# Sums over heads taken for two groups at a time, in a six-layer attention stack on one core

## The chip, the cores and the metric

The kernel runs on one core of a Trainium2 chip. The metric is the device time of one execution in microseconds (us). Times of a kernel before and after a change are taken in turns on the same chip.

## The reference

Eight sequences of 512 positions with 128 features go through six layers, and then through a gated FFN. What one layer computes (H = 16 heads of 8 features, biases and the affine parts of the norms left in):

```python
q = (h @ wq.T + bq).reshape(bh, sl, H, DH)
k = (h @ wk.T + bk).reshape(bh, sl, H, DH)
scores = einsum('blhd,bmhd->bhlm', q, k) / sqrt(DH)
w_avg = softmax(scores, -1).mean(axis=1)          # mean over the 16 heads
new_w = softmax(w_avg + exp(-|l - m| / 16), -1)
sa = einsum('blm,bme->ble', new_w, h)
h1 = ln(h + sa, l1w, l1b)
h2 = ln(h1, l2w, l2b)
ff = relu(h2 @ w1.T + b1) @ w2.T + b2
h = ln(h2 + ff, l3w, l3b)
```

The stack's input is the normalised x, its output is added to x. The FFN of 128 to 512 features (silu gate, two 512x512 layers with gelu, back to 128) is then added too. All arithmetic is float32 in its inputs and outputs.

## The kernel before

A **unit** is one layer of one sequence: 6 x 8 = 48 units, in the order of the layers, so that a sequence comes back after eight units. A unit has 32 **steps** (`PAIRS`). In each step PE computes two blocks of scores, [128, 512] each (`ps`, one PSUM bank each, from a ring of six, L385); DVE takes the maximum of every row (`top`, L394); ACT the exponential with its row sum (`e`, `zs`, L399). A row of a block is one position and one head: 32 positions x 4 heads fill the 128 partitions.

Two steps make a **group** (`Group`): four blocks, one `e` tile, for 128 positions (`lc`) and four heads (`turn`). Four groups, eight steps, make the 16 heads of a query chunk. What follows for a group that began its second step at s:

- s + 2: DVE takes reciprocals of the row sums (`r`, L408), POOL spreads them into a [128, 32] weight for each block (`rp`, L410).
- s + 5: the **gather** (L420). Four float32 products, each in its own 32 columns of TensorE, sum each block of `e` over its four heads, weighted by `rp`, into the one PSUM tile `acc`. The four groups of a query chunk accumulate there.
- After the fourth group only: at s + 5 ACT takes the exponential of `acc` (`w`, `mix_exp`, L427); at s + 8 PE transposes it (`pt_w`, L193) and DVE multiplies it by the decay (`wT`, L437); at s + 10 PE multiplies it with h (`po`, L445), and DVE scales and adds h (L453, L454).

Counted in the unit's steps, gathers stand at every even step, `w` at 4, 12, 20, 28, `pt_w` at 7, 15, 23, 31, `po` at 1, 9, 17, 25.

The other work of neighbouring units is spread over the same steps by hand: `plan_before` (K and Q projections `pk`, `pq` at steps 3 and 5 with their ACT results `kT`, `qT`, splits, stacking by DMA on SP), `plan_after` (three norms, the hidden layer `pf` at 11, 13, 19, 21 with its relu `g`, L338, and the MLP output `py`, L348, in two halves at 27 and 29, each added to `z` by DVE, L355), and `plan_turns` (transposes `pt_h`, `pt_u` at the end of step 31, copied by ACT to `hT`, `uT`). `norm_c` is the norm of the sum with the MLP output: statistics of two chunks (L172), and of two more later. The steps of one unit's MLP lie two units after its scores.

The order on every engine is thus written out: `at(step, place, fn)` appends work to the list of an engine in a step, `first` puts it in front. Within a step PE gets its two scores, then the list; DVE its two maxima, then the list; ACT the list, then its two exponentials. Engines wait for each other by semaphores alone.

Buffers: `pk`, `pq`, `pf`, `py`, `pt_w` and `po` share one PSUM bank (`one`, pool `ps_one`). `e` has four tiles, the score ring six banks.

After the last unit come eight passes of the FFN (`gated`, one for each sequence, the next one's input prepared within it by `gated_in`), with the leftover steps of the last units between their parts.

Of the kernel before, what the change touches and what calls it, by code (L numbers as in the profile page):

```python
# [9 lines left out]
F32 = mybir.dt.float32  # L10
# [7 lines left out]
P = 128  # L18
# [3 lines left out]
QB = 32  # L22
# [7 lines left out]
def attn_stack_then_ffn(ctx: ExitStack, tc: tile.TileContext, a: dict, out: bass.AP):  # L30
    nc = tc.nc
    ctx.enter_context(tc.manual_schedule())
    x = a["x"]
    B, L, E = x.shape
# [4 lines left out]
    LC = L // P  # L39
    FC = F // P  # L40
    HC = HID // P
    NB = P // QB
# [4 lines left out]
    wts = ctx.enter_context(tc.tile_pool(name="wts", bufs=1))  # L47
    state = ctx.enter_context(tc.tile_pool(name="state", bufs=1))
    proj = ctx.enter_context(tc.tile_pool(name="proj", bufs=2))
    epool = ctx.enter_context(tc.tile_pool(name="e", bufs=4))  # L50
    work = ctx.enter_context(tc.tile_pool(name="work", bufs=2))
    small = ctx.enter_context(tc.tile_pool(name="small", bufs=6))
    ps_big = ctx.enter_context(tc.tile_pool(name="ps_big", bufs=6, space=PSUM))
# [39 lines left out]
    x_in = {}  # L93

    def load_x(b, n):
        t = state.tile([P, LC, E], F32, tag="x", name=f"x_{n}", bufs=3)
        nc.sync.dma_start(t, x[b].rearrange("(c p) e -> p c e", p=P))
        return t

# [90 lines left out]
    def transpose(pt, src):  # L190

        for c in range(LC):
            nc.tensor.transpose(pt[:, c * P : (c + 1) * P], src[:, c, :], ident)  # L193
# [10 lines left out]
    PAIRS = LC * STRIPS * 2  # L204

    class Unit:
# [12 lines left out]

        def turn_h(self, pt):  # L220
            transpose(pt, self.h[:, :, 0:E])
            self.hT = work.tile([P, L], F32, tag="hT", name=f"hT_{self.n}")
            return lambda: nc.scalar.copy(self.hT, pt)

        def project_k(self):
# [141 lines left out]
    class Group:  # L367
# [38 lines left out]
        def weights(self):  # L406
            r = small.tile([P, NB], F32, tag="r", name=f"r_{self.n}")
            nc.vector.reciprocal(r, self.zs)  # L408
            self.rp = small.tile([P, NB, QB], F32, tag="rp", name=f"rp_{self.n}", bufs=4)
            nc.gpsimd.tensor_tensor(  # L410
                self.rp,
                pick.unsqueeze(1).to_broadcast([P, NB, QB]),
                r.unsqueeze(2).to_broadcast([P, NB, QB]),
                ALU.mult,
            )
# [7 lines left out]
                )  # L423

        def mix_exp(self):
            self.w = work.tile([P, LC, P], F32, tag="w", name=f"w_{self.n}")
            nc.scalar.activation(  # L427
                self.w.rearrange("p c l -> p (c l)"), acc, AF.Exp, scale=1.0 / H
            )
# [31 lines left out]
    PE_, DVE_, ACT_, RING_ = range(4)  # L461
    later = {}

    def at(step, place, fn):
        later.setdefault((step, place), []).append(fn)

    def first(step, place, fn):
        later.setdefault((step, place), []).insert(0, fn)
# [11 lines left out]
    def norm_steps(base, un, make, s0, s1, s2, s3, s4):  # L480

        at(base + s0, DVE_, lambda: (make(), un.ln.stats(0, 2)))
        at(base + s1, DVE_, lambda: un.ln.stats(2, LC))
        at(base + s2, DVE_, lambda: un.ln.aggregate())
        at(base + s3, DVE_, lambda: un.ln.centre())
        at(base + s4, DVE_, lambda: un.ln.scale())
# [32 lines left out]
    def plan_after(un):  # L519

        s = (un.u + 1) * PAIRS
        norm_steps(s, un, un.norm_a, 11, 12, 13, 14, 15)
        at(s + 16, DVE_, lambda: un.affine_a(0))
        at(s + 17, DVE_, lambda: un.affine_a(1))
        norm_steps(s, un, un.norm_b, 19, 20, 22, 23, 24)
        at(s + 25, DVE_, lambda: un.affine_b(0))
        at(s + 26, DVE_, lambda: un.affine_b(1))
        s += PAIRS
        for f, step in enumerate((11, 13, 19, 21)):
            matmuls(s + step, lambda f=f: un.hidden(f))  # L530
        for half, step in enumerate((27, 29)):
            at(s + step, PE_, lambda half=half: un.mlp_out(half))
            at(s + step, DVE_, lambda half=half: un.mlp_add(half))
        norm_steps(s, un, un.norm_c, 28, 30, PAIRS, PAIRS + 9, PAIRS + 10)
        at(s + PAIRS + 11, DVE_, lambda: un.affine_c(0))
        at(s + PAIRS + 12, DVE_, lambda: un.affine_c(1))

    def plan_group(gr, s):

        first(s + 2, DVE_, gr.weights)  # L540
        first(s + 5, PE_, gr.gather)
        if gr.turn == STRIPS - 1:
            at(s + 5, ACT_, gr.mix_exp)
            at(s + 8, PE_, gr.mix_turn)
            at(s + 8, DVE_, gr.mix_decay)
            at(s + 10, PE_, gr.mix_values)
            at(s + 10, DVE_, gr.mix_end)
# [10 lines left out]
    for s in range(-2 * PAIRS, 0):  # L558
# [4 lines left out]
        step_rest(s)  # L563
        step_ring(s)

    for u, un in enumerate(obj):
        un.z1 = work.tile([P, LC, E], F32, tag="z1", name=f"z1_{un.n}")
        if u + 2 < B:
            x_in[u + 2] = load_x(u + 2, f"in{u + 2}")
        if un.b == 4 and un.d + 1 < D:  # L570
            load_layer(un.d + 1)
        if u == U - B:
            load_ffn()
            xs = {0: load_x(0, "out0")}
        if u + 2 < U:
            plan_before(obj[u + 2])
        plan_turns(u)
        plan_after(un)
        for pr in range(PAIRS):
            s = u * PAIRS + pr  # L580
            lc, turn, half = pr // 8, (pr // 2) % STRIPS, pr % 2
            if half == 0:
                gr = Group(un, lc, turn)
            peak, exps = gr.scores(half)
            if half == 1:
                plan_group(gr, s)
            pending(s, PE_)
            peak()
            pending(s, DVE_)
            pending(s, ACT_)  # L590
            exps()
            step_ring(s)
# [13 lines left out]
    def gated_in(b):  # L606

        xb = xs.pop(b)
        nc.gpsimd.tensor_tensor(xb, xb, hs[b][:, :, 0:E], ALU.add)
        if b + 1 < B:  # L610
            xs[b + 1] = load_x(b + 1, f"out{b + 1}")
        v = work.tile([P, LC, E], F32, tag="vf", name=f"v_{b}", bufs=1)
        ln = Norm(xb, v, f"f{b}")
        ln.stats(0, LC)
        ln.aggregate()
        ln.centre()
        ln.scale()
        yield
        vT = work.tile([P, L], F32, tag="hT", name=f"vT_{b}")
        pt = transposed(v, f"v{b}")  # L620
        nc.scalar.copy(vT, pt)  # L621
        ready[b] = (xb, vT)

    def gated(b):
        xb, vT = ready.pop(b)
        ahead = gated_in(b + 1) if b + 1 < B else iter(())
        gg = epool.tile([P, HC, L], F32, tag="e", name=f"fg_{b}")
        for o in range(HC):
            sl = slice(o * P, (o + 1) * P)
            p1, p2 = ring([P, L], f"p1_{b}_{o}"), ring([P, L], f"p2_{b}_{o}")  # L630
            nc.tensor.matmul(p1, fw1[:, sl], vT, start=True, stop=True)
            nc.tensor.matmul(p2, fw2[:, sl], vT, start=True, stop=True)
            sil = work.tile([P, L], F32, tag="w", name=f"sil_{b}_{o}")
            nc.scalar.activation(sil, p1, AF.Silu, scale=cols["f_w1s_col"][:, o : o + 1])
            nc.vector.scalar_tensor_tensor(
                gg[:, o, :], p2, cols["f_w2s_col"][:, o : o + 1], sil, ALU.mult, ALU.mult
            )
            yield
        for wt, sc, nm in ((fh1, "f_h1s_col", "h1"), (fh2, "f_h2s_col", "h2")):
            g2 = epool.tile([P, HC, L], F32, tag="e", name=f"{nm}_{b}")  # L640
            for o in range(HC):
                ph = ring([P, L], f"p{nm}_{b}_{o}")
                for c in range(HC):
                    nc.tensor.matmul(  # L644
                        ph, wt[:, c, o * P : (o + 1) * P], gg[:, c, :],
                        start=(c == 0), stop=(c == HC - 1),
                    )
                nc.scalar.activation(g2[:, o, :], ph, AF.Gelu, scale=cols[sc][:, o : o + 1])
                if (nm, o) in (("h1", HC - 1), ("h2", HC - 1)):
                    next(ahead, None)  # L650
                yield
            gg = g2
        po = ring([P, LC, E], f"fo_{b}")
        for c in range(LC):
            for k in range(HC):
                nc.tensor.matmul(  # L656
                    po[:, c, :], gg[:, k, c * P : (c + 1) * P], fw3[:, k, :],
                    start=(k == 0), stop=(k == HC - 1),
                )
        y = work.tile([P, LC, E], F32, tag="z1", name=f"y_{b}")  # L660
        nc.vector.tensor_tensor(y, po, fw3s.unsqueeze(1).to_broadcast([P, LC, E]), ALU.mult)  # L661
        nc.gpsimd.tensor_tensor(y, y, xb, ALU.add)  # L662
        nc.sync.dma_start(out[b].rearrange("(c p) e -> p c e", p=P), y)

    for _ in gated_in(0):
        pass
# [66 lines left out]
```

## Time and profile before

| | us |
|---|---|
| median of 3 runs | 2818.68 (2818.52 to 2821.95) |
| profiled execution: time | 2825.2 |
| profiled execution: span from the first to the last instruction | 2823.4 |
| PE busy | 2746.7 |
| ACT busy | 2496.5 |
| DVE busy | 2393.9 |
| POOL busy | 1801.2 |
| granted TensorE clock | 0.998 of full speed |

In the profile a busy time is a sum over the span, and PE's includes modelled ends of matmuls. A row of a group gives its busy time, the mean of one instruction in ns, and after the bar the idle time of the engine just before it, with what ended the most of it. A timeline row gives start and length in us, engine, line, operation, output and inputs, shapes and the number of merged instructions; idle time ahead of it stands in brackets with its releaser. Float32 products appear as two matmul instructions each, so a gather is eight.

### The profile page before, as it was taken

How to read it: one execution, taken by the hardware profiler on the slowest of the kernel's cores; microseconds unless marked ns; L12 is line 12 of the kernel's file. 1: busy time of each engine (PE TensorE's matmuls, PEld its weight loads, DVE VectorE, ACT ScalarE, POOL GpSimd, SP SyncE). 2: the span in 40 equal slices, each digit the busy share in tenths (PEclk: the TensorE clock that was granted, in tenths of full speed). 3: DMA queues.
4: the chain of work that ended last, by engine and by line, in shares of the span. 5: the costliest groups of instructions: out<-in, count | busy, mean ns of one | idle time of the engine just before them, and what ended most of it. 6: DMA issues, size and time to landing. Idle time of an engine off the chain costs nothing.

```text
span 2823.4 us, 51628 instructions
## 1 busy us (share of the span) xinstructions
PE 2746.7 (97%) x14944; PEld 1370.0 (49%) x14944; DVE 2393.9 (85%) x5942; ACT 2496.5 (88%) x6845; POOL 1801.2 (64%) x2205
## 2 busy tenths in 40 slices
PE   5999999999999999999999999999999999989999
PEld 2444545445454454454544545445445454445554
DVE  4999999999999999999999999999999999921110
ACT  5999999999999999999999999999999999933232
POOL 4668776776766767767677676676776767633210
PEclk9999999999999999999999999999999999999999
DMA  5555444544544445444454454454564444300000
GB/s 117 114 118 132 93 104 104 112 108 106 111 105 107 97 113 115 110 92 103 105 127 104 93 113 106 103 120 94 117 153 95 102 105 110 78 8 8 15 12 8
DMA packets 133387, 271.06 MB, mean 96 GB/s; under 512 B 39024, under 2 KB 56560, under 8 KB 133104
## 3 DMA queue, kind: packets, MB, share of 16 engines
q1 hardware_dynamic: 131808, 267.73, 42.3%
q8 instruction: 119, 1.95, 0.3%
q14 instruction: 164, 1.34, 0.2%
q10 hardware_dynamic: 1296, 0.03, 0.0%
HBM read 13.86 MB, written 2.10 MB: 6 GB/s over the span
## 4 chain that ended last, share of the span: by engine, by line
PE 47%; ACT 22%; DVE 18%; POOL 6%; issue 5%; DMA 0%; SPq 0%; POOLq 0%; ACTq 0%; DVEq 0%
ACT e L399 19%; DVE top L394 14%; PE ps L385 13%; PE acc L420 12%; PE py L348 6%; PE ph L644 6%; PE po L445 3%; PE pk L229 1%; ACT w L427 1%; POOL z L306 1%; PE pq L238 1%; POOL rs_a L178 1%; POOL z L186 1%; POOL z L181 1%; ACT g L338 1%
## 5 line engine op out<-in xcount | busy, mean ns | idle before, releaser
L399 ACT ACTIVATE e<-ps,top 128x512 f32<-128x512 f32 x3072 | 2134.5, 840 | 23.9 <-DVE top L394 20.4
L394 DVE TENSOR_REDUCE top<-ps 128x1 f32<-128x512 f32 x3072 | 1952.5, 682 | 42.9 <-PE ps L385 35.8
L385 PE MATMUL ps<-ks,qs 128*128 128x512 f32 x3072 | 1240.0, 477 | 34.2 <-ACT e L399 26.0
L399 ACT ACTIVATION_READ_ACCUMULATOR e<-ps,top 128x1 f32 x3072 | 1103.5, 359 | 0.0
L385 PEld LDWEIGHTS ps<-ks,qs 128*128 128x128 f32 x3072 | 495.4, 189 | 888.3 <-ACT e L399 661.6
L420 PE MATMUL acc<-e,rp 128*32 128x512 f32 x6144 | 819.1, 605 | 0.8 <-POOL rp L410 0.3
L410 POOL TENSOR_TENSOR rp<-pick,r 128x128 f32<-128x128 f32 x768 | 308.1, 401 | 549.8 <-DVE r L408 265.8
L420 PEld LDWEIGHTS acc<-e,rp 128*32 128x32 f32 x6144 | 121.0, 108 | 263.1 <-issue 126.5
L278 POOL TENSOR_TENSOR m<-hiq,mask 128x512 f32<-128x512 f32 x192 | 245.2, 1277 | 4.8 <-DMA qs<-m 4.8
L278 POOL TENSOR_TENSOR m<-loq,mask 128x512 f32<-128x512 f32 x192 | 245.1, 1277 | 2.6 <-DMA qs<-m 2.6
L445 PEld LDWEIGHTS po<-h,wT 128*128 128x128 f32 x1536 | 201.0, 191 | 18.9 <-DVE wT L437 1.5
L445 PE MATMUL po<-h,wT 128*128 128x129 f32 x1536 | 202.7, 275 | 0.7 <-DVE wT L437 0.7
L336 PE MATMUL pf<-uT,w 128*128 128x512 f32 x384 | 195.8, 591 | 0.0
L348 PEld LDWEIGHTS py<-w,g 128*128 128x128 f32 x1536 | 186.2, 192 | 10.9 <-ACT vT L621 1.1
L348 PE MATMUL py<-w,g 128*128 128x128 f32 x1536 | 186.9, 275 | 0.8 <-ACT vT L621 0.8
L338 ACT ACTIVATE g<-pf,b_col 128x512 f32<-128x512 f32 x192 | 168.2, 876 | 2.2 <-PE pf L336 2.2
L661 DVE TENSOR_TENSOR y<-fo,fw3s 128x512 f32<-128x512 f32 x8 | 5.5, 692 | 175.8 <-PE fo L656 175.8
L427 ACT ACTIVATE w<-acc 128x512 f32<-128x512 f32 x192 | 134.2, 699 | 22.6 <-PE acc L420 22.6
L662 POOL TENSOR_TENSOR y<-y,x_out 128x512 f32<-128x512 f32 x8 | 10.1, 1265 | 199.7 <-DVE y L661 199.7
L408 DVE RECIPROCAL r<-zs 128x4 f32<-128x4 f32 x768 | 130.9, 170 | 5.7 <-ACT e L399 0.3
L437 DVE TENSOR_TENSOR wT<-pt_w,decay 128x512 f32<-128x512 f32 x192 | 126.9, 661 | 4.5 <-PE pt_w L193 4.2
L355 DVE TENSOR_TENSOR z<-py,z 128x256 f32<-128x256 f32 x96 | 40.8, 425 | 105.3 <-PE py L348 105.3
(97 smaller groups left out, 2637.3 us busy)
## 6 DMA issues: line engine op xcount, KB each, us to landing
qs<-m SPq DMA_DIRECT2D x1536, 128.0 KB, 2.4
ks<-hik SPq DMA_DIRECT2D x384, 64.0 KB, 2.0
ks<-lok SPq DMA_DIRECT2D x384, 64.0 KB, 2.0
rows<-in_rows SPq DMA_DIRECT2D x6, 448.0 KB, 5.1
x_in<-in_x SPq DMA_DIRECT2D x8, 256.0 KB, 3.1
x_out<-in_x SPq DMA_DIRECT2D x8, 256.0 KB, 3.1
out<-y SPq DMA_DIRECT2D x8, 256.0 KB, 2.4
w<-in_w1t SPq DMA_DIRECT2D x6, 256.0 KB, 2.9
```

Of the source, the lines that this page charges most:

```text
L278: nc.gpsimd.tensor_tensor(m[:, lc - 2 * two], part.unsqueeze(2).to_broadcast([P, NB, PER_STRIP, QB]), mask.unsqueeze(1).to_broadcast([P, N ...
L336: nc.tensor.matmul(pf, w1[:, f * P : (f + 1) * P], self.uT, start=True, stop=True)
L338: return lambda: nc.scalar.activation(self.g[:, f, :], pf, AF.Relu, bias=cols["b1_col"][:, k : k + 1])
L348: nc.tensor.matmul(self.py[:, k, :], self.g[:, f, c * P : (c + 1) * P], w2[:, f, :], start=(f == 0), stop=(f == FC - 1),)
L385: nc.tensor.matmul(ps[s], qs[:, nb * P : (nb + 1) * P].bitcast(F32R), un.ks[:, i, :].bitcast(F32R), start=True, stop=True,)
L394: nc.vector.tensor_reduce(top[s], ps[s], AX.X, ALU.max, negate=True)
L399: nc.scalar.activation(self.e[:, nb, :], ps[s], AF.Exp, bias=top[s], accum_out=self.zs[:, nb : nb + 1],)
L410: nc.gpsimd.tensor_tensor(self.rp, pick.unsqueeze(1).to_broadcast([P, NB, QB]), r.unsqueeze(2).to_broadcast([P, NB, QB]), ALU.mult,)
L420: nc.tensor.matmul(acc[nb * QB : (nb + 1) * QB, :], self.rp[:, nb, :], self.e[:, nb, :], start=(self.turn == 0), stop=(self.turn == STRIPS ...
L427: nc.scalar.activation(self.w.rearrange("p c l -> p (c l)"), acc, AF.Exp, scale=1.0 / H)
L445: nc.tensor.matmul(self.po, self.wT[:, c, :], self.unit.h[:, c, 0 : E + 1], start=(c == 0), stop=(c == LC - 1),)
L644: nc.tensor.matmul(ph, wt[:, c, o * P : (o + 1) * P], gg[:, c, :], start=(c == 0), stop=(c == HC - 1),)
```

## The change

Groups are planned with a list `pair`. A group's reciprocals and weights stay where they were. Its gather is not placed until the second group of the pair is planned; then both gathers are put in the second one's step s + 5, one behind the other. So gathers stand at steps 0, 4, 8, ... 28, two at each. `w`'s exponential remains at the second group's s + 5, after the fourth group as before.

The additions of the MLP output move from steps 27 and 29 to 28 and 30, and the first statistics of `norm_c` from 28 to 29.

Because `e` and `rp` live longer, `e` gets five buffers and `rp` six. Room for that comes from `hT` and `w` with one buffer in place of two, `x` with two in place of three, and from the FFN part, whose `v` takes the tag `m0` and whose `sil` takes `wT`. The FFN's inputs are loaded two ahead: the first two before the passes, and each later one behind the store of the output two before it.

```diff
-    epool = ctx.enter_context(tc.tile_pool(name="e", bufs=4))
+    epool = ctx.enter_context(tc.tile_pool(name="e", bufs=5))
...
-        t = state.tile([P, LC, E], F32, tag="x", name=f"x_{n}", bufs=3)
+        t = state.tile([P, LC, E], F32, tag="x", name=f"x_{n}", bufs=2)
...
-            self.hT = work.tile([P, L], F32, tag="hT", name=f"hT_{self.n}")
+            self.hT = work.tile([P, L], F32, tag="hT", name=f"hT_{self.n}", bufs=1)
...
-            self.rp = small.tile([P, NB, QB], F32, tag="rp", name=f"rp_{self.n}", bufs=4)
+            self.rp = small.tile([P, NB, QB], F32, tag="rp", name=f"rp_{self.n}", bufs=6)
...
-            self.w = work.tile([P, LC, P], F32, tag="w", name=f"w_{self.n}")
+            self.w = work.tile([P, LC, P], F32, tag="w", name=f"w_{self.n}", bufs=1)
...
             at(s + step, PE_, lambda half=half: un.mlp_out(half))
-            at(s + step, DVE_, lambda half=half: un.mlp_add(half))
-        norm_steps(s, un, un.norm_c, 28, 30, PAIRS, PAIRS + 9, PAIRS + 10)
+            at(s + step + 1, DVE_, lambda half=half: un.mlp_add(half))
+        norm_steps(s, un, un.norm_c, 29, 30, PAIRS, PAIRS + 9, PAIRS + 10)
...
-    def plan_group(gr, s):
+    def plan_group(pair, gr, s):
...
         first(s + 2, DVE_, gr.weights)
-        first(s + 5, PE_, gr.gather)
+        pair.append(gr)
+        if len(pair) == 2:
+            two = tuple(pair)
+            pair.clear()
+            first(s + 5, PE_, lambda: [x.gather() for x in two])
         if gr.turn == STRIPS - 1:
             at(s + 5, ACT_, gr.mix_exp)
...
-            xs = {0: load_x(0, "out0")}
+            xs = {b: load_x(b, f"out{b}") for b in range(2)}
...
-        if b + 1 < B:
-            xs[b + 1] = load_x(b + 1, f"out{b + 1}")
-        v = work.tile([P, LC, E], F32, tag="vf", name=f"v_{b}", bufs=1)
+        v = work.tile([P, LC, E], F32, tag="m0", name=f"v_{b}", bufs=1)
...
-            sil = work.tile([P, L], F32, tag="w", name=f"sil_{b}_{o}")
+            sil = work.tile([P, L], F32, tag="wT", name=f"sil_{b}_{o}")
...
         nc.sync.dma_start(out[b].rearrange("(c p) e -> p c e", p=P), y)
+        if b + 2 < B:
+            xs[b + 2] = load_x(b + 2, f"out{b + 2}")
```

More of the change, by code (lines that the diff above doesn't have):

```diff
@@ L564, in attn_stack_then_ffn @@
         step_ring(s)
+    pair = []
     for u, un in enumerate(obj):
@@ L585, in attn_stack_then_ffn @@
             if half == 1:
-                plan_group(gr, s)
+                plan_group(pair, gr, s)
             pending(s, PE_)
@@ L618, in gated_in @@
         yield
-        vT = work.tile([P, L], F32, tag="hT", name=f"vT_{b}")
+        vT = work.tile([P, L], F32, tag="hT", name=f"vT_{b}", bufs=1)
         pt = transposed(v, f"v{b}")
```

## The prediction

> **What bounds the kernel now.** I read the page first: engine shares, chain, the idle column of the groups. Three engines are nearly full, and the chain that ended last changes engine all the time (PE 47%, ACT 22%, DVE 18%), so the busy shares do not name a bound. Two idle times point at one place: ACT waits 46 times for the sum `acc`, and DVE 96 times for the MLP output `py`. 46 is the number of the 48 units that have an MLP in their steps.
>
> ```profile
> PE 2746.7 (97%) x14944; PEld 1370.0 (49%) x14944; DVE 2393.9 (85%) x5942; ACT 2496.5 (88%) x6845; POOL 1801.2 (64%) x2205
> L427 ACT ACTIVATE w<-acc 128x512 f32<-128x512 f32 x192 | 134.2, 699 | 22.6 <-PE acc L420 22.6
> L355 DVE TENSOR_TENSOR z<-py,z 128x256 f32<-128x256 f32 x96 | 40.8, 425 | 105.3 <-PE py L348 105.3
> ```
>
> Then the timeline of one unit, engine by engine. PE waits for ACT at 1497.21 (second score of step 24) and again at 1548.21, the same place one unit later: a unit takes 51.0 us. The PE rows from there (start, length, line, what):
>
> ```profile
> 1497.21 0.51 PE L385 MATMUL ps<-ks,qs 128*128 128x512 f32 x1 [0.17 <-ACT e L399]
> 1497.65 1.07 PE L420 MATMUL acc<-e,rp 128*32 128x512 f32 x8
> 1498.64 0.74 PE L385 MATMUL ps<-ks,qs 128*128 128x512 f32 x2
> ...
> 1501.67 0.73 PE L385 MATMUL ps<-ks,qs 128*128 128x512 f32 x2
> 1502.24 1.95 PE L348 MATMUL py<-w,g 128*128 128x128 f32 x16
> 1503.94 0.70 PE L385 MATMUL ps<-ks,qs 128*128 128x512 f32 x2
> 1504.57 1.06 PE L420 MATMUL acc<-e,rp 128*32 128x512 f32 x8
> ...
> 1510.05 0.60 PE L193 MATMUL pt_w<-ident,w 128*128 128x128 f32 x4
> ```
>
> No row after the first has a wait until 1523.45: PE sets the pace over steps 24 to 39. ACT is the bound of the rest: from step 35 to step 27 of the next unit it issues an exponential every 0.665 us without a gap. Where PE is dense, ACT and DVE lose time:
>
> ```profile
> 1505.70 0.60 ACT L427 ACTIVATE w<-acc 128x512 f32<-128x512 f32 x1 [0.49 <-PE acc L420]
> 1509.24 0.69 ACT L399 ACTIVATE e<-ps,top 128x512 f32<-128x512 f32 x1 [0.25 <-DVE top L394]
> 1517.62 0.69 ACT L230 ACTIVATE kT<-pk,bk_col 128x512 f32<-128x512 f32 x1 [0.21 <-PE pk L229]
> 1504.22 0.43 DVE L355 TENSOR_TENSOR z<-py,z 128x256 f32<-128x256 f32 x1 [0.64 <-PE py L348]
> ```
>
> A unit's ACT work is 64 exponentials x 0.67 + 4 `w` x 0.48 + 8 others x 0.57 = 49.4 us. So ACT loses 1.6 us of 51.0, nearly all between steps 28 and 36. That is the most that any change off ACT can gain: 48 x 1.6 = 77 us.
>
> **What the Trainium skill says.** "TensorEngine Tiling (Array Packing)", Key Properties: changing the tiling mode drains TensorE. The trace agrees. A gather (128x32 tiles) starts its first four matmuls, then the second four 0.45 later (1526.91, 1527.36), and the next score starts 0.99 after the first: 2 x 0.45 plus 0.09. The two scores behind it take 0.57 to the next start (0.66 in the chain), those that follow a 128x128 matmul 0.44 to 0.47. "TensorE: Matmul & The Clock Gate", Architectural detail: ACT and DVE are strict FIFO and matmuls keep their order. The trace agrees: behind the `w` that waits at 1505.70, an exponential whose `top` was ready stands too. "Perfetto Trace Analysis", Tensor Engine Instruction: ends of matmuls are modelled, so I work with starts.
>
> **The change, part by part.**
>
> *Gathers in pairs.* The changed program's instruction order shows eight gather matmul pairs together at steps 0, 4, 8, ... 28 instead of four at every even step. Work is the same; one entry and exit of the 128x32 mode is saved per pair. By starts: four scores, gather, four scores, gather took 2 x (1.22 + 0.99) = 4.42; paired it is 8 scores at 0.22 + 0.23 for mode and weights + 0.99 + 0.87 = 3.85 to 4.05. PE saves about 0.37 a pair, 3 us a unit. In the stretch that ACT bounds this is worth nothing.
>
> In the PE stretch it is bunched wrongly. Step 24 starts when ACT frees a score bank, in both kernels. Before, PE then runs gathers 24, 26, 28 up to the end of step 28; after, both sums of step 24 and both of 28, four in place of three (the fourth was done at step 22, in PE's slack). From 1497.21: 0.44 + 1.85 (pair) + 0.57 + 0.81 (`po`) + 0.92 (scores 26, 27) = `py` at 1501.8, 0.4 earlier than before; + 1.70 + 0.63 + 1.85 = end of the pair at 1506.1, against 1505.57. `w` stays in step 28 and so starts at 1506.18: **ACT +0.48**. Queued behind it are the exponentials of step 28.
>
> *MLP addition one step later.* DVE no longer waits 0.64 and 0.61 for `py`; but the maxima of step 28 wait for scores that PE issues behind `py`, so DVE is 0.1 us better at best. Those of step 29 wait for the pair (1506.1 + 0.5 from score start to maximum = 1506.6; before 1506.15). Second `py`: 1506.67 to 1508.37, before 1506.14 to 1507.84. Now the new wait: `py` and `pt_w` share the one bank of `ps_one`. The second addition stands behind two maxima of step 30 (from 1508.85, 0.6 each, then 0.35), ending at 1510.4. PE has no gather at step 30 any more and reaches `pt_w` at 1509.3. **PE stalls 1.1 us**, with `pt_h`, `pt_u`, the scores of step 32 and the next pair behind it: `pt_w` at 1510.5 for 1510.05.
>
> Followed on: maxima of step 31 from 1510.75 (before 1510.05); `hT` on ACT at 1512.8 (1512.10); pair at step 32 from 1512.4 to 1514.3; maxima of step 33 from 1514.8 (13.45 before); of 34 from 1516.55 (15.18); exponentials of 34 from 1517.3 (15.95); `kT` 1518.6 (17.62); `w` of step 36 at 1520.5 (19.53). PE itself reaches `pk` at 1516.55 for 1516.50: its saving just pays for its stall, but ACT is **1.0 us later**, and from here ACT is full to the next step 27 and gets nothing back.
>
> *Pairs in ACT's stretch.* Scores behind a pair come 0.87 later. DVE's lead over ACT there is 0.43 (step 42) to 1.6 us. I find a DVE wait of 0.6 at step 41 and 0.4 at 49, and `w` of step 52 with 0.1 to spare: 0 to 0.4 us a unit lost. The trace before does not show a pair; I take 0.05 and keep both ends.
>
> *Buffers.* `e` 5: a pair frees its first buffer two steps before reuse, as now. `w` 1: read at step 7, written again at 12, 8 us on. `hT` 1: read by step 5, written at 31. `x` 2: loads (3.1 us) are two units apart; in the FFN part the load of b+2 follows the store of b on SP and is read a whole pass later (some 40 us). `rp` 6, `vf` on `m0` and `sil` on `wT` meet no live tile. All nil under that cover; without it 3.1 us a load, 25 us at most. The FFN part is PE without gaps; there ACT gains one table load (1.28 us) and leftovers shift by a few places, covered by PE; some us either way without it. In the units no POOL instruction changes place, and on SP only the `x` loads do.
>
> *Sum.* 46 units x (1.0 + 0.05) = +48 us. Against the profiled execution (span 2823.4, time 2825.2) that is 2873; this execution is 6.5 us above the median 2818.7, so the median becomes **2866 us**, +1.7%.
>
> **Rivals.**
> 1. *The saved mode changes reach the end (not slower).* In steps 24 to 39 four pairs save 4 x 0.37 = 1.5 us of PE, in the stretch where PE paces. If DVE, freed of its 1.25 us of waits for `py`, gets the additions out before PE needs the bank, and the `w` delay is made up from the 0.33 us by which `kT` waited and the 0.5 us by which exponentials 30 and 31 were late, ACT's loss falls from 1.6 to 0.9: 46 x 0.7 = 32, 2786 us; all of it gone is 2742. It decides if PE stalls at `pt_w` under 0.4 us. For it: PE has most work in the page. Against: the order of DVE, where the addition comes after both maxima. 24%.
> 2. *Even.* +0.48 at `w` and the savings cancel because PE's arrival at `pk` is unchanged: 2815 to 2824 us. 5%.
> 3. *DVE becomes the bound too.* Its work is 49.2 us a unit; waits of 0.4 to 0.8 at all eight pairs eat its lead and ACT loses 0.5 more a unit: 46 x 1.5 = 69, 2888 us. For it: leads of 0.43 us. Against: ACT's exponentials, recorded 0.68 long when alone, grow to 1.08 before step 28: 0.4 us of queued work. 15%.
> 4. *The pairs are not back to back.* Excluded by the instruction order.
>
> **How the numbers follow.** Main case 56%, its own range 2838 to 2882 (0.4 to 1.35 us a unit); rival 3 15%; so slower 0.71, within 0.2% (5.6 us, about what a measurement of this kernel tells from no change) 0.05, faster 0.24. The range takes in rival 3 and most of rival 1: 2776 to 2894; left out are the ends of rivals 1 and 3, some 15%.
>
> **What would show it.** Right: one unit takes 52.0 us; `w` of step 28 waits for `acc` some 0.9 us (idle of L427 near 45 in place of 22.6); PE idle at L193 `pt_w` released by DVE L355, about 1.1 x 46 = 50 us; DVE idle at L394 released by L385 well above 35.8; L355 idle nearly gone outside the tail; gathers at 1.85 a pair. Wrong: no PE idle at `pt_w`, or ACT idle below 1.6 us a unit, or a pair much shorter than 1.8 us.

## The result, and the profile after

| | before | after |
|---|---|---|
| median, us | 2819.26 (4 runs) | 2898.98 (4 runs) |
| profiled execution, us | 2825.2 | 2898.9 |
| span of the profile, us | 2823.4 | 2897.2 |
| one unit in the profile (median), us | 51.00 | 52.51 |

The changed kernel is slower: ratio 1.028, 95% interval 1.0265 to 1.0295. Of the 73.7 us between the profiled executions, 72 lie between the first exponential of the first unit and the last one of the last unit. The other 6 us between the medians are there because the profiled execution of before was that much above its own median, and the one of after was not. Only one execution of before was profiled, so where in it those 6 us lay is not known.

In the page before, DVE's maxima waited little for scores (after the bar: idle time of the engine ahead of the group, and what ended the most of it):

```profile
L394 DVE TENSOR_REDUCE top<-ps 128x1 f32<-128x512 f32 x3072 | 1952.5, 682 | 42.9 <-PE ps L385 35.8
```

In the page after, with the other two groups whose waits grew (the additions, L355, have dropped off the page):

```profile
L394 DVE TENSOR_REDUCE top<-ps 128x1 f32<-128x512 f32 x3072 | 1935.6, 679 | 187.7 <-PE ps L385 187.0
...
L193 PE MATMUL pt_w<-ident,w 128*128 128x128 f32 x768 | 124.1, 284 | 62.2 <-DVE z L355 51.3
L427 ACT ACTIVATE w<-acc 128x512 f32<-128x512 f32 x192 | 117.2, 610 | 53.1 <-PE acc L420 53.1
```

From the changed kernel's list of waits (us in total, times, longest):

```profile
PE pt_w L193 <- DVE z L355: 51.3, 46, 1.1
ACT e L399 <- DVE top L394: 50.5, 102, 7.4
...
DVE z L355 <- PE py L348: 37.5, 2, 21.3
```

DVE's wait for `py` is gone but for two in the end part. In its place stand three others: PE waits 46 times for the addition, 1.1 us each; DVE waits for scores, 187 us where it was 36; ACT waits for `acc` ahead of `w`, 53 us where it was 23. Below is the timeline of a unit in the same layer as the one shown before, PE first, from the second score of step 24, which ACT releases. A product of a gather, of `py` or of `po` appears as two instructions, a score as one; so x4 are the scores of two steps.

```profile
1488.14 0.50 PE L385 MATMUL ps<-ks,qs 128*128 128x512 f32 x1 [0.17 <-ACT e L399]
1488.58 1.92 PE L420 MATMUL acc<-e,rp 128*32 128x512 f32 x16
...
1491.82 1.16 PE L385 MATMUL ps<-ks,qs 128*128 128x512 f32 x4
1492.93 2.02 PE L348 MATMUL py<-w,g 128*128 128x128 f32 x16
1494.71 0.71 PE L385 MATMUL ps<-ks,qs 128*128 128x512 f32 x2
1495.35 1.92 PE L420 MATMUL acc<-e,rp 128*32 128x512 f32 x16
1497.20 0.73 PE L385 MATMUL ps<-ks,qs 128*128 128x512 f32 x2
...
1501.77 0.63 PE L193 MATMUL pt_w<-ident,w 128*128 128x128 f32 x4 [1.12 <-DVE z L355]
```

Counted from the first row, the scores of step 29, behind the pair of step 28, come at 9.06 (before 8.36), `pt_w` at 13.63 (before 12.84). A pair takes 1.85 us from its start to that of the next score. On the other two engines:

```profile
1497.74 1.29 DVE L394 TENSOR_REDUCE top<-ps 128x1 f32<-128x512 f32 x2 [0.90 <-PE ps L385]
1506.06 1.29 DVE L394 TENSOR_REDUCE top<-ps 128x1 f32<-128x512 f32 x2 [0.59 <-PE ps L385]
1497.40 0.60 ACT L427 ACTIVATE w<-acc 128x512 f32<-128x512 f32 x1 [1.14 <-PE acc L420]
1502.76 0.69 ACT L399 ACTIVATE e<-ps,top 128x512 f32<-128x512 f32 x1 [0.53 <-DVE top L394]
1508.57 0.69 ACT L399 ACTIVATE e<-ps,top 128x512 f32<-128x512 f32 x1 [0.33 <-DVE top L394]
1511.80 0.62 ACT L427 ACTIVATE w<-acc 128x512 f32<-128x512 f32 x1
```

The maxima of steps 29 and 33 stand behind the pairs of steps 28 and 32 (0.90 and 0.59), the exponentials of steps 31 and 34 behind late maxima. The last row is `w` of step 36, 23.66 us after the first row. In the unit of the kernel before it stood 22.32 us after its own first row (1497.21):

```profile
1519.53 0.60 ACT L427 ACTIVATE w<-acc 128x512 f32<-128x512 f32 x1
```

So 1.34 of the 1.5 us that a unit loses are lost in these twelve steps.

### The profile page after: what moved, and what is told of

It is laid out like the page before. It is cut to its first block, busy times and chain, and to the rows that moved or that the text cites. A ratio compares the mean times of both kernels' runs of the same rounds, so it can differ in the third digit from the quotient of the medians.

```text
span 2897.2 us, 51535 instructions
## 1 busy us (share of the span) xinstructions
PE 2729.9 (94%) x14944; PEld 1419.0 (49%) x14944; DVE 2382.6 (82%) x5942; ACT 2509.9 (87%) x6846; POOL 1798.8 (62%) x2205
## 3 DMA queue, kind: packets, MB, share of 16 engines
q14 instruction: 164, 1.34, 0.2%
## 4 chain that ended last, share of the span: by engine, by line
ACT 39%; PE 38%; DVE 13%; issue 8%; POOL 1%; DMA 0%; SPq 0%; POOLq 0%; ACTq 0%; DVEq 0%
ACT e L399 33%; PE acc L420 11%; DVE top L394 10%; PE ps L385 8%; PE py L348 6%; PE ph L648 6%; ACT g L338 3%; ACT w L427 2%; PE po L445 2%; PE pt_w L193 1%; ACT kT L230 1%; PE p L635 1%; DVE z L454 1%; PE p L636 1%; ACT qT L239 1%
## 5 line engine op out<-in xcount | busy, mean ns | idle before, releaser
L399 ACT ACTIVATE e<-ps,top 128x512 f32<-128x512 f32 x3072 | 2082.7, 729 | 62.9 <-DVE top L394 50.5
L385 PE MATMUL ps<-ks,qs 128*128 128x512 f32 x3072 | 1178.3, 469 | 62.4 <-ACT e L399 49.7
L385 PEld LDWEIGHTS ps<-ks,qs 128*128 128x128 f32 x3072 | 524.8, 189 | 697.2 <-ACT e L399 476.9
L399 ACT ACTIVATION_READ_ACCUMULATOR e<-ps,top 128x1 f32 x3072 | 761.2, 248 | 0.0
L420 PE MATMUL acc<-e,rp 128*32 128x512 f32 x6144 | 739.6, 599 | 0.0
L420 PEld LDWEIGHTS acc<-e,rp 128*32 128x32 f32 x6144 | 160.4, 109 | 353.3 <-issue 254.8
L193 PE MATMUL pt_w<-ident,w 128*128 128x128 f32 x768 | 124.1, 284 | 62.2 <-DVE z L355 51.3
L427 ACT ACTIVATE w<-acc 128x512 f32<-128x512 f32 x192 | 117.2, 610 | 53.1 <-PE acc L420 53.1
L193 PEld LDWEIGHTS pt_w<-ident,w 128*128 128x128 f32 x768 | 81.0, 140 | 124.8 <-issue 70.1
L338 ACT ACTIVATE g<-pf,b_col 128x512 f32<-128x512 f32 x192 | 135.6, 706 | 3.1 <-PE pf L336 3.1
```

What stands on the lines that cost most here:

```text
L338: return lambda: nc.scalar.activation(self.g[:, f, :], pf, AF.Relu, bias=cols["b1_col"][:, k : k + 1])
L385: nc.tensor.matmul(ps[s], qs[:, nb * P : (nb + 1) * P].bitcast(F32R), un.ks[:, i, :].bitcast(F32R), start=True, stop=True,)
L399: nc.scalar.activation(self.e[:, nb, :], ps[s], AF.Exp, bias=top[s], accum_out=self.zs[:, nb : nb + 1],)
L420: nc.tensor.matmul(acc[nb * QB : (nb + 1) * QB, :], self.rp[:, nb, :], self.e[:, nb, :], start=(self.turn == 0), stop=(self.turn == STRIPS ...
L427: nc.scalar.activation(self.w.rearrange("p c l -> p (c l)"), acc, AF.Exp, scale=1.0 / H)
```

## The experiments

Each is timed in turns with the kernel before on the same chip; times are medians.

**1. Both additions back** (on the changed kernel)

```diff
-            at(s + step + 1, DVE_, lambda half=half: un.mlp_add(half))
-        norm_steps(s, un, un.norm_c, 29, 30, PAIRS, PAIRS + 9, PAIRS + 10)
+            at(s + step, DVE_, lambda half=half: un.mlp_add(half))
+        norm_steps(s, un, un.norm_c, 28, 30, PAIRS, PAIRS + 9, PAIRS + 10)
```

> Pairs kept; both additions of the MLP output back in the steps of their py (27, 29), first statistics back at 28. Theory (the late addition holds the shared bank, PE stands 1.1 us at pt_w of step 31, and the pair at step 32 and the maxima of step 33 follow late): PE idle at pt_w gone, a unit about 0.9 us shorter than in the changed kernel, 46 x 0.9 = 41, some 2858 us. Rival A (pairs starve DVE wherever they stand, the place of the addition is a side matter): 2890 to 2900 us. Rival B (w waiting for the pair of step 28 is what costs): 2890 to 2900 us, w still waits 0.9 or more.

Measured 2859.58 us, ratio to before 1.0142 (1.0125 to 1.0159). The place of the additions is worth 39 of the 80 us while gathers are paired. PE passes step 31 without a wait (the first row is the second score of step 24):

```profile
1465.88 0.50 PE L385 MATMUL ps<-ks,qs 128*128 128x512 f32 x1 [0.17 <-ACT e L399]
...
1477.21 1.17 PE L385 MATMUL ps<-ks,qs 128*128 128x512 f32 x4
1478.22 0.60 PE L193 MATMUL pt_w<-ident,w 128*128 128x128 f32 x4
```

Counted from the first row `pt_w` stands at 12.34, earlier even than before (12.84). A unit takes 51.66 us.

**2. Only the second addition back** (the first in step 28, the second in 29; the first statistics stay in step 29)

> Pairs kept; only the second addition back in step 29, the first one stays in step 28. Theory: pt_w waits for the second half's bank alone, so this is as good as having both back, within 5 us of it (some 2858 us). If the first half's place matters too (it delays the maxima of step 29 or frees those of step 28), the two differ by more than 5 us. Rivals A and B: 2890 to 2900 us.

Measured 2878.06 us, 1.0208 (1.0193 to 1.0224): half of what experiment 1 won, where a difference within 5 us was expected. PE does not wait at `pt_w` here either. DVE, behind the second addition, does the first half's statistics too, which before stood in step 28:

```profile
1488.32 0.42 DVE L355 TENSOR_TENSOR z<-py,z 128x256 f32<-128x256 f32 x1 [0.64 <-PE py L348]
1488.66 0.48 DVE L172 BATCH_NORM_STATS2 st_c<-z 128x6 f32<-128x128 f32 x2
1489.05 1.27 DVE L394 TENSOR_REDUCE top<-ps 128x1 f32<-128x512 f32 x2
```

So it is not the bank alone, as theory had it: 0.39 us of statistics moved ahead of the maxima of step 30 go with another 0.38 us a unit (52.04 for 51.66). That cost does not carry over to the changed kernel. There the same statistics are done while DVE waits for the scores of step 30 anyway; what stands in the way is the second addition, ahead of the maxima of step 31:

```profile
1499.03 0.45 DVE L172 BATCH_NORM_STATS2 st_c<-z 128x6 f32<-128x128 f32 x2
1500.00 1.29 DVE L394 TENSOR_REDUCE top<-ps 128x1 f32<-128x512 f32 x2 [0.51 <-PE ps L385]
1501.20 0.41 DVE L355 TENSOR_TENSOR z<-py,z 128x256 f32<-128x256 f32 x1
1501.65 0.49 DVE L172 BATCH_NORM_STATS2 st_c<-z 128x6 f32<-128x128 f32 x2
1502.06 1.27 DVE L394 TENSOR_REDUCE top<-ps 128x1 f32<-128x512 f32 x2
```

Counted over ACT's usual pitch of 0.664 us, the exponentials of step 31 are 0.64 us late in the changed kernel and 0.18 in experiment 1; those of steps 33 and 34, behind the pair that PE's wait puts off, 0.65 and 0.18 in sum. So the late addition costs about as much by DVE's order as by PE's wait.

**3. `w`'s exponential one step later** (on the changed kernel)

```diff
-            at(s + 5, ACT_, gr.mix_exp)
+            at(s + 6, ACT_, gr.mix_exp)
```

> The changed kernel with w's exponential one step later (29, 5, 13, 21), nothing else. Theory: the exponentials from step 30 on wait for maxima that stand behind PE's second py, not for w, so taking away w's wait of 1.1 us brings nothing: 2894 to 2900 us. Rival B (w's wait holds ACT, and ACT is full from step 36 on): ACT idle at w falls from 53 us to under 10 and the time by 46 x 0.5 to 1.1 = 23 to 50 us, 2850 to 2876 us.

Measured 2898.31 us, 1.0281 (1.0266 to 1.0297): no gain, although the wait is gone from its group:

```profile
L427 ACT ACTIVATE w<-acc 128x512 f32<-128x512 f32 x192 | 120.2, 626 | 0.1
```

ACT waits for maxima instead, 0.38 and 0.86 us in steps 29 and 30 of the unit looked at:

```profile
1497.40 0.69 ACT L399 ACTIVATE e<-ps,top 128x512 f32<-128x512 f32 x1 [0.38 <-DVE top L394]
1499.71 0.69 ACT L399 ACTIVATE e<-ps,top 128x512 f32<-128x512 f32 x1 [0.86 <-DVE top L394]
```

The most visible new wait of ACT is thus not what costs. As the trace reads, the path runs from PE's pair over its second `py` to DVE.

**4. Late additions alone** (the edit of experiment 1 the other way round, on the kernel before)

> The kernel before (single gathers, all its buffers) with the additions in steps 28 and 30 and the statistics at 29, 30. Theory: with the gather of step 30 between, PE comes to pt_w at about the moment the addition ends, so no stall or a small one; maxima of step 31 come 0.2 us later: 2819 to 2828 us. If the late addition is bad by itself: PE idle at pt_w of 0.5 us or more a unit and 2840 us or more.

Measured 2832.28 us, 1.0046 (1.0031 to 1.0061): 13 us, 4 above the expected range. With the single gather of step 30 between, PE reaches `pt_w` about when the bank is free: no wait there is in the profile's list. The exponentials of step 31 are 0.64 us late here too, by DVE's order; those of steps 33 and 34 are not:

```profile
1514.72 0.69 ACT L399 ACTIVATE e<-ps,top 128x512 f32<-128x512 f32 x1 [0.53 <-DVE top L394]
```

Alone the moved additions cost 13 us and the pairs 40; together 80. The missing 26 are their meeting: without a gather in step 30 PE comes early to a bank that is held late. The 0.47 us at steps 33 and 34 make some 22 of them (an estimate, 46 x 0.47).

**5 and 6. Pairs only in one stretch.** Both are made from the changed kernel and keep its buffers; number 5 has the additions early as well, number 6 late. `slot` is the step of the pair (0 stands for 32); the groups named keep single gathers:

```diff
         pair.append(gr)
+        slot = (s + (7 if gr.turn % 2 == 0 else 5)) % PAIRS
+        if slot in (24, 28, 0):        # experiment 6: not in
+            pair.clear()
+            first(s + 5, PE_, gr.gather)
```

> Pairs only at steps 4, 8, 12, 16, 20, where ACT sets the pace; at 22 to 32 single gathers, and the additions early as in the kernel before. Theory (the loss is made where PE sets the pace; in ACT's stretch pairs cost the 0.2 us a unit that the traces show between w of step 36 and step 24): 48 x 0.2 = 10, 2824 to 2834 us. Rival A (pairs cost wherever they stand): five eighths of the 40 us that pairs with early additions cost, 2840 to 2850 us.

Measured 2819.91 us, 1.0005 (0.9996 to 1.0013): no difference, where 2824 us or more were expected. All the new buffers are in this kernel, so they do not cost by themselves.

> The counterpart: pairs only at steps 24, 28 and 32, single gathers elsewhere, additions late as in the changed kernel. Theory: nearly all of the loss stays, 2884 to 2896 us. Rival A: three eighths of the pairs' cost and the 13 us of the late additions, about 2850 us.

Measured 2899.35 us, 1.0286 (1.0271 to 1.0301): the whole loss, 3 us above the expected range. The five pairs in ACT's stretch cost and bring nothing in sum; the three at 24, 28 and 32, with the late additions, are all of it.

**7 and 8. The transposes `pt_h` and `pt_u` away from step 31.** Number 7 is the kernel before with this, number 8 has the pairs and early additions (the lines that replace the old ones):

```diff
+        if 0 <= u + 2 < U:
+            h_step = 17 if obj[u + 2].d else PAIRS - 1
+            at(u * PAIRS + h_step, RING_, lambda: obj[u + 2].turn_h(ring([P, L], f"pt_h{u + 2}")))
+        if 0 <= u - 1 < U:
+            at(u * PAIRS + PAIRS + 6, RING_, lambda: obj[u - 1].turn_u(ring([P, L], f"pt_u{u - 1}")))
```

> The kernel before with other work taken out of the stretch in which PE sets the pace: the transpose pt_h moved from step 31 to step 17 (not for the first eight units) and pt_u from step 31 to step 6 of the next unit, their copies on ACT with them; gathers single, additions early. Theory (ACT's loss of 1.6 us a unit comes from PE's surplus of work in steps 24 to 36): 0.88 us of PE and 1.1 us of ACT leave the stretch, ACT's work in all is the same, so 0.3 to 0.9 us a unit is won, 2776 to 2805 us. If ACT's loss has another cause: within 6 us of the kernel before.

Measured 2851.62 us, 1.0115 (1.0100 to 1.0130): slower, a miss. The relief of PE was real, but where ACT used to copy `hT` and `uT` it now waits for maxima:

```profile
1526.34 0.69 ACT L399 ACTIVATE e<-ps,top 128x512 f32<-128x512 f32 x1 [0.47 <-DVE top L394]
...
1529.52 0.69 ACT L399 ACTIVATE e<-ps,top 128x512 f32<-128x512 f32 x1 [0.33 <-DVE top L394]
```

Both, at steps 32 and 34, are new against the kernel before. The 1.1 us of copies had filled a gap of ACT; moved, they lie in the stretch where ACT has none: up to `w` of step 36 a unit gains 0.45 us (21.86 for 22.31), behind it it loses 1.07 (29.76 for 28.69). So a surplus of PE's work alone does not explain ACT's loss there: DVE's maxima are late too.

> Pairs everywhere with early additions, and pt_h and pt_u moved as in the run before this one. Theory: the pair at step 28 still delays the second py by 0.5 us, but PE can make it up behind step 31; the gap to the kernel with moved transposes and single gathers shrinks below the 40 us of unmoved ones, to 10 (the 0.2 us a unit of ACT's stretch) to 30: 2795 to 2835 us. If pairs pay once PE is less full: below the kernel with moved transposes alone.

Measured 2895.33 us, 1.0272 (1.0255 to 1.0289). The gap to number 7 is 44 us, not 10 to 30: pairs do not pay when PE has less to do either.

**9, 10, 11. One pair undone at a time**, with early additions (`slot == 24`, `28`, `0` in the edit of number 5; all pairs: 2859.58).

> Pairs everywhere except for the two groups of step 24 (gathers at 22 and 24, single, as before); additions early. Theory (the pair at 24 carries the gather of step 22 into the stretch in which PE sets the pace, and 26 is saved only later): from step 24 on PE now runs three gathers up to the end of step 28, as before, and saves one mode change; first py 1.2 us earlier, second py 0.37 us earlier, w of 28 at least 0.3 us earlier. So not slower than before, and up to 0.8 us a unit faster: 2780 to 2822 us. If the pair at 28 itself costs (w and the maxima of step 29 behind two gathers): 2840 to 2860 us, near the 2860 us of all pairs with early additions.

Measured 2836.29 us, 1.0062 (1.0049 to 1.0074): 23 us better than all pairs, yet 17 slower than before and 14 above the expected range. PE came early, as expected, but had to wait at a score of step 27, since the ring of six banks was full:

```profile
1456.93 0.50 PE L385 MATMUL ps<-ks,qs 128*128 128x512 f32 x1 [0.17 <-ACT e L399]
1457.27 1.95 PE L348 MATMUL py<-w,g 128*128 128x128 f32 x16
...
1459.60 1.92 PE L420 MATMUL acc<-e,rp 128*32 128x512 f32 x16
```

The time of the gather missing at 26 could not be spent, and the pair of step 28 brings that gather in behind the wait. It is the mechanism of step 24 once more, three steps on. Against experiment 5, which has the same pairs in ACT's stretch, `w` of step 36 is 0.31 us later (22.28 for 21.97), which is all that a unit loses.

> Pairs everywhere except at 28 (single gathers at 26 and 28), so that the pair at 24 is kept between them; additions early. Theory: four gathers in the stretch up to step 28 as with all pairs, and one mode change more; second py 0.85 us later than before in place of 0.48: 2865 to 2890 us. If the pair at 28 is what costs: 2819 to 2835 us.

Measured 2868.54 us, 1.0173 (1.0159 to 1.0187): undoing only the pair of step 28 makes it worse, as expected.

> Pairs everywhere except at step 32 (single gathers at 30 and 32); additions early. Theory: second py and w as with all pairs, so most of the 40 us stays; the scores of step 33 come earlier relative to their pair, PE does one mode change more: 2850 to 2870 us. If the pair at 32, which keeps the maxima of step 33 waiting, is what costs: 2819 to 2835 us.

Measured 2852.82 us, 1.0121 (1.0106 to 1.0137): most of the loss stays.

**12. The pairs that do no harm, later layers only** (the edit of number 5, with `or gr.unit.d == 0` in its condition)

> Pairs only at steps 4 to 20, and only in layers 2 to 6 (the first layer's units keep single gathers throughout); additions early. With such pairs in all layers a unit of the later layers took 50.84 us in its profile for 51.00 in the kernel before, and one of the first layer 51.24 for 51.05. If that difference is the pairs', 40 units x 0.16 = 6 us are won: 2811 to 2815 us. If it is only the profile's or is given back in the end part: within 2.5 us of the kernel before.

Measured 2820.28 us for 2821.19 of before, 0.9996 (0.9988 to 1.0005): no difference, so no version here beats the kernel before.

## Why the prediction was right or wrong

The direction was right, and so was the place of most of the loss; the size was not. 48 us were forecast, 80 measured, 5 us above the range. The step that failed is the "1.0 us later" at step 36: it was 1.34, because `pt_w` came 0.34 us later than forecast; about half of that is a wait of PE for the shared bank that was put at nothing. The 0.05 for pairs in ACT's stretch was too small as well. A unit with an MLP lost 1.52 us and not 1.05, which is 70 us for 46 of them; some 4 lie in the other units and the ends, and 6 in the profiled execution.

- **PE's pace from step 24 and the fourth gather**: right. Experiments 6 and 9 to 11 place the loss there, and undoing the pair of step 24 is worth the most of the three.
- **The wait of PE at `pt_w`**: right, 1.12 us for 1.1, 51.3 us in all for 50.
- **A wait for the same bank at the first `py`**: put at nothing. `py` takes the bank over from `po`, and DVE reads `po` behind the maxima of step 25, which wait 0.48 us behind the pair of step 24. This is that read in the unit shown:

```profile
1492.43 0.35 DVE L454 SCALAR_TENSOR_TENSOR z<-po,rw,h 128x128 f32<-128x128 f32 x1
```

It ends at 1492.78, and `py` starts 0.15 us later, as `pt_w` does after the addition; before, the read had ended 1.24 us ahead of `py`. Now `py` starts 0.34 us after the last score, where 0.23 is usual, and takes 1.78 to the next start, where 1.70 was forecast: 0.18 us of PE. Experiments 1, 2, 3, 6, 8 and 11 show the same; those with a single gather at 24 or 26 (4, 5, 7, 9, 10 and 12) do not.
- **Saving of a mode change**: mis-sized. By starts, steps 25 to 28 took 8 scores in 2.43 and two gathers in 1.98 before; after, 2.32 and 1.85: 0.24 us a pair, not 0.37. Besides, the terms listed for the end of the pair of step 28 add up to 1505.98, not 1506.1. The scores behind it came 0.70 late in place of 0.5 (0.4 by its own terms), and `pt_w` 0.79 in place of 0.45.
- **"ACT +0.48" at `w`**: `w`'s wait was there (53 us), but it is no loss. Experiment 3 takes it away for nothing. The same delay of PE reaches ACT over the second `py` and the maxima.
- **"ACT is 1.0 us later" at step 36**: mis-sized, 1.34. The exponential of step 34 was 1.69 later where 1.35 was forecast, and this 0.34 is what `pt_w` was later than forecast.
- **"0.4 us of queued work" in ACT**: wrong as slack. I read it from rows that grow from 0.68 to 1.08 us, and set it against late maxima. In the changed kernel the exponentials of steps 26, 42 and 50 started some 0.25 us late each, and the rows of that stretch grow to 0.80 only. The first of these costs nothing, since ACT then waits 1.14 us at `w`; the other two count in ACT's stretch.
- **Pairs in ACT's stretch**, 0.05 us a unit: too small for the stretch, and the way back is not what I wrote. From `w` of step 36 to the next step 24 a unit takes 28.88 us in the changed kernel and 28.69 before. Experiments 1, 2, 5 and 9 to 12, which have these pairs, take 28.88 to 28.90, and 4 and 6, which have none, 28.59, so the 0.2 us are theirs. Yet experiment 5 loses no time, and 6 is as slow as the changed kernel: without these pairs its `w` of step 36 stands at 23.97 in place of 23.63. In all runs step 24 starts 0.14 us after the end of the exponential that frees its bank, and with these pairs that exponential's row is shorter (0.75 for 1.00), so PE comes earlier against ACT:

```profile
1496.07 1.00 ACT L399 ACTIVATE e<-ps,top 128x512 f32<-128x512 f32 x1
1487.25 0.75 ACT L399 ACTIVATE e<-ps,top 128x512 f32<-128x512 f32 x1
```

The first is this row in the unit before, the second in the unit after. That the one pays for the other is read from the traces, not tried.
- **Buffers**: nil by experiment 5. The new order of the FFN's loads shows as three waits of POOL for `x_out`, 10.8 us in all, but behind the last exponential the changed kernel is only 0.6 us longer.
- **The number of units**: 46 were counted, for the MLP. Between the first scores of successive units, 40 of the 47 lengths grew by 1.5 us each, four by 1.8 to 1.9, the first three by 0.7, 0.4 and 1.6. Against 46 x 1.05 the size of the term is the miss, not the count.
- **Median against profile**: I moved the profiled execution's 6.5 us over its median to both kernels. The changed kernel's was on its median, and 6 us of the miss are that.
- **Rival 1** (savings reach the end) fell: even with PE relieved (8) or with one pair fewer (9) pairs lost. **Rival 3** (DVE starved at all eight pairs) came near the time, but not by its way. DVE does wait behind the pairs of steps 40 and 48 as well (0.36 and 0.47 us), but experiment 5 has these waits too and loses no time.

## What to carry to other kernels

Where an engine is held by a full ring of buffers, other work done just before the hold ends costs nothing; putting that work off, be it to save a switch, moves it behind the hold and onto the path. Before batching, mark for each stretch which engine waits, and batch only in the stretch where the batched engine has slack; there, expect little from it (here nothing). A step put off holds its buffer longer: count who takes that buffer next and when, and test the two edits apart, since here 13 and 40 us became 80.

## What was not expected of the hardware

PE started 0.14 to 0.15 us after the end of the row that released it: the second score of step 24 after ACT's exponential in all fourteen profiles, `pt_w` and the first `py` after DVE's row. Where it had waited for DVE like this, its 128x128 work was a little dearer by starts: `py` took 1.78 us in place of 1.70, four transposes of `pt_w` 0.46 in place of 0.43. The wait at `py` was too short to stand in the profile's list.

ACT's rows that overlap and lengthen are no measure of slack: exponentials started late by the delay of their maxima although the rows just ahead were 0.1 us longer than alone, and those behind kept the pitch of 0.66 us. The length is real for whoever waits for the end: PE's score started 0.14 us after it whether the row was 0.75 or 1.00 us long.
